# Moving six image measurements to VectorE, combining six more images and reordering the fifth one in a group-norm convolution

## The chip, the cores and the metric

The kernel runs on one core of a Trainium2 chip. The metric is the device time of one execution in microseconds (us). All runs of this study are marked fast in the record (none fell into a slower state), so they may be compared with each other. Single executions of one kernel lie up to about 2 us either side of its median. Part of that has one visible cause: the weights land at a slightly different time in each run, and the whole program shifts with them. Where traces are compared below, times are therefore also given *from the first product*, which is TensorE's first instruction, issued as soon as the range of the weights is known (17.71 us after the start of the span in the trace of before, 16.86 to 19.39 us in the others).

## The reference, cut to what matters

160 images of 128 channels and 32 x 32 pixels, five sets of weights of 32 images each, quantised in two levels on the way in. Every image is normalised per group of four channels, convolved 3 x 3, and added to itself.

```python
def _gn(v, G=32, eps=1e-5):
    g = v.reshape(B_, G, C_ // G, H_, W_)
    m = jnp.mean(g, axis=(2, 3, 4), keepdims=True)
    s = jnp.var(g, axis=(2, 3, 4), keepdims=True)
    return ((g - m) / jnp.sqrt(s + eps)).reshape(v.shape)

x = x + _L0_conv_ref(_gn(x), L0_conv_U)   # w = v1 + v2, two levels of floor()
```

## The kernel before

Every image is split into a high and a low float16 part, and TensorE convolves both. *Direct* images are normalised first (ScalarE: `z`, `hi`), and VectorE takes the low part and the row differences and sums (`lo`, `rows`). *Combined* images take differences and sums of rows first (`v`) and split afterwards (`vh` on ScalarE, `vl` on VectorE), which needs fewer products. Each image's mean and variance must be measured many steps ahead:

```python
def image(self, j, image):                 # by VectorE
    # ... half is 512 elements; st and both are small tiles
    for h in range(2):
        self.nc.vector.bn_stats(st[:, h, :], image[:, h * half : (h + 1) * half])
    self.nc.vector.bn_aggr(both, st)
    # ... two tiny products into mv

def image_sum(self, j, image, junk):       # by ScalarE, first pass
    self.nc.scalar.activation(junk, image, ACTF.Copy, scale=-1.0 / image.shape[1], accum_out=...)
def image_square(self, j, image, junk):    # by ScalarE, second pass
    self.nc.scalar.activation(junk, image, ACTF.Square, bias=..., accum_out=...)

def by_vector(self, i):
    return i >= self.EARLY and i % 8 in self.MEASURED      # MEASURED = (): nobody
def combined(self, i):
    return self.STEADY <= i < self.imgs - LAST and i % 8 in self.COMBINED   # STEADY = 14, LAST = 4
```

Step i finishes the convolution of image i. It begins with the products for the *next* image's sums of row pairs, into the one PSUM tile `m`. ScalarE copies half of it out (`leave`), VectorE makes the even and odd rows of the output from both halves (`pairs`, two instructions), and only then may TensorE overwrite `m` or go on with that image:

```python
def conv(self, i, on_the_way):
    if i + 1 < self.imgs:
        self.sums_of_pairs(i + 1)                # into m
    for halves in ((0,), (1,)) if i == self.imgs - 1 else ((0, 1),):
        for col in self.COLS:
            ...
            self.rest_of_column(i, col, halves)  # into eo

def leave(self, i):
    self.nc.scalar.copy(m2, self.m[i][:, 1])     # "m<-m" on ScalarE
def pairs(self, i):
    # ... m and m2 from leave(); rows are the even and odd rows of eo
    nc.vector.tensor_add(rows[:, :, 0], m[:, 0], m2)   # "eo<-m,m" on VectorE
    nc.vector.tensor_sub(rows[:, :, 1], m[:, 0], m2)
```

So a step's start needs, in this order: TensorE's sums, ScalarE's copy, VectorE's two instructions. The engines work through their queues in order, and what stands ahead of these in a queue delays TensorE.

Of the kernel before, what the change touches and what calls it, by code (L numbers as in the profile page):

```python
# [22 lines left out]
LAST = 4  # L23
# [109 lines left out]
def run(steps):  # L133

    while True:
        try:
            next(steps)
        except StopIteration as end:
            return end.value
# [170 lines left out]
class Main:  # L310
# [23 lines left out]

    STAT_LEAD = 14
    LOAD_LEAD = 20
    STEADY = 14
    COMBINED = (1, 3, 5, 7)
    MEASURED = ()
    EARLY = 8  # L340
    FIRST = 3

# [4 lines left out]
    def __init__(self, tc, ctx, keep, x, u, out):  # L347
        nc = self.nc = tc.nc
        self.imgs, C, self.H, self.W = x.shape
        P = self.P = nc.NUM_PARTITIONS  # L350
        assert C == P and self.H * self.W == 1024
        self.per_set = self.imgs // N_SETS
        self.xv = x.rearrange("(b n) c h w -> n c b (h w)", n=N_SETS)
        self.ov = out.rearrange("(b n) c h w -> n c b (h w)", n=N_SETS)
        self.uv = u.rearrange("n (o i k) -> n o i k", o=C, k=TAPS)

        def pool(name, bufs, **kw):
            return ctx.enter_context(tc.tile_pool(name=name, bufs=bufs, **kw))

        self.const = pool("const", 1)  # L360
        self.qpool = pool("quant", 1)
        self.wpool = pool("weights", 2)
        self.upool = pool("u", 1)
        self.xpool = pool("x", 12)
        self.zpool = pool("z", 3)
        self.parts = pool("parts", 4)
        self.rows = pool("rows", 4)
        self.wide = pool("wide", 1)
        self.wide_parts = pool("wide_parts", 2)
        self.evac = pool("evac", 2)  # L370
        self.sums = pool("sums", 4)
        self.unread = pool("unread", 1)
        self.small = pool("small", 3)
        self.ps_eo = pool("ps_eo", 2, space=PSUM)
        self.ps_m = pool("ps_m", 1, space=PSUM)
        self.ps_stat = pool("ps_stat", 1, space=PSUM)
        self.ps_tr = pool("ps_tr", 1, space=PSUM)
        self.steps = Steps(nc, keep)
        self.chunks, self.z, self.hi, self.v, self.eo, self.m = {}, {}, {}, {}, {}, {}
        self.sum = {}  # L380
        self.wts = {}
        self.columns = []

        cuts = [0, 2, 4, 8, 12, *range(16, self.imgs + 1, 8)]
        self.groups = [range(a, b) for a, b in zip(cuts, cuts[1:])]
        self.group_of = {i: k for k, g in enumerate(self.groups) for i in g}
        self.stats = {}
# [95 lines left out]


    def by_vector(self, i):
        return i >= self.EARLY and i % 8 in self.MEASURED

    def measure(self, i, stages=(0, 1)):

# [31 lines left out]

    def combined(self, i):

        return self.STEADY <= i < self.imgs - LAST and i % 8 in self.COMBINED

    def column_of(self, i):

# [95 lines left out]
    def banks(self, pool, tag, i):  # L623
        return pool.tile([self.P, 2, self.H // 2, self.W], F32, tag=tag, name=f"{tag}{i}")

    def direct_hi(self, i, col):

        if i not in self.eo:
            self.eo[i] = self.banks(*((self.ps_eo, "eo") if i < 2 else (self.ps_m, "m")), i)
        self.taps(i, (self.hi[i], 0), col, self.eo[i], False)  # L630
# [35 lines left out]
    def conv(self, i, on_the_way):  # L666


        if i + 1 < self.imgs:
            self.sums_of_pairs(i + 1)  # L670

        for halves in ((0,), (1,)) if i == self.imgs - 1 else ((0, 1),):
            for col in self.COLS:
                if col != self.COLS[0]:
                    on_the_way(col)
                self.rest_of_column(i, col, halves)
        del self.v[i]
# [64 lines left out]
    def run(self):  # L742
# [16 lines left out]
        warm = self.const.tile([P, 1], F32, tag="warm", name="warm")  # L759
# [22 lines left out]
        def take(steps, count):  # L782
            for _ in range(count):
                next(steps, None)
# [5 lines left out]
        def parts(i):  # L790
            self.normalise(i)
            self.high_part(i)
# [21 lines left out]
        measure(1, 3)  # L814
        self.stats[1].means()
        self.stats[1].deviations()
        parts(0)
        self.stats[1].variances()
        self.stats[1].deviation()
# [37 lines left out]
        for i in range(self.imgs):  # L857
            n, b = self.place(i)


            def on_the_way(col):
                if col == self.COLS[1]:
                    for st in ready:
                        st.means()
                    for *column, parts in self.columns:
                        turned.append((column, self.turn_column(*column, parts)))
                    self.columns.clear()
                if col == self.COLS[2]:
                    for st in middle:
                        st.variances()  # L870

            if i < self.FIRST:
                if i == self.FIRST - 1:
                    self.sums_of_pairs(self.FIRST)

                j = (i - 1) % self.FIRST
                self.direct_hi(j, self.COLS[2])
                self.direct_lo(j, self.COLS[2])
                if i == 0:
                    self.stats[2].variances()  # L880
                    self.stats[2].deviation()
                    self.stats[2].scales()
                for col in self.COLS:
                    on_the_way(col)
            else:
                j = i - 1
                self.conv(i, on_the_way)
            ahead = i + min(10 + i // 2, self.STAT_LEAD + 1)
            to_measure = range(measured, min(self.imgs, ahead))
            measured += len(to_measure)  # L890
            if n + 1 < N_SETS:
                if b == (2 if n == 0 else 0):
                    self.load_set(n + 1)
                if b == (4 if n == 0 else 2):
                    later = (s for col in self.COLS for s in self.make_column(n + 1, col))
            by_scalar = [k for k in to_measure if not self.by_vector(k)]


            direct = self.FIRST < i + 2 < self.imgs and not self.combined(i + 2)
            if i < self.FIRST:  # L900
                self.residual(j)
                if i == self.FIRST - 1:
                    self.leave(i + 1)
                    self.pairs(i + 1)
            if self.combined(i + 2):
                self.low_combined(i + 2)
            if direct:
                self.low_part(i + 2)
            take(later, 1)
            if direct:  # L910
                self.combinations(i + 2)
            if i > self.FIRST and self.by_hand(j):
                self.residual(j)
            for k in by_scalar:
                self.measure(k, (0,))
            if i > self.FIRST and not self.by_hand(j):
                self.residual(j)
                self.accumulate(j)
            if self.combined(i + 4):
                self.outer_rows(i + 4)  # L920


            if self.FIRST < i + 1 < self.imgs:
                self.leave(i + 1)
            if self.combined(i + 3):
                self.high_combined(i + 3)
            elif self.FIRST < i + 3 < self.imgs:
                self.normalise(i + 3)
                self.high_part(i + 3)
            for k in by_scalar:  # L930
                self.measure(k, (1,))
            for st in middle:
                st.deviation()
                st.scales()
            for st in ready:
                st.deviations()
            for column, pt in turned:
                self.keep_column(*column, pt)
            turned = []


            if self.FIRST < i + 1 < self.imgs:
                self.pairs(i + 1)
            if self.combined(i + 4):
                self.combine(i + 4)
            else:
                take(later, 1)
            if b == self.per_set - 4:
                run(later)

            middle, ready = ready, []
            for k in to_measure:
                if self.by_vector(k):
                    self.measure(k)
                group = self.group_of[k]
                if k + 1 == self.groups[group].stop:
                    ready.append(self.stats[group])
            self.store(i - 2)
            while loaded * NB < min(self.imgs, i + self.LOAD_LEAD):
                self.load(loaded)  # L960
                loaded += 1
# [49 lines left out]
```

## Time and profile before

| | before |
|---|---|
| time, median | 1011.69 us (1011.02 to 1012.54) |
| span of the profiled run | 1007.8 us |

In the profile PE is TensorE, PEld its loading of weights, DVE VectorE, ACT ScalarE and POOL GpSimd. The busy shares of the page (time, share, instructions), and two stretches of the first images, from the table of stretches of before (length, then busy time of PE, PEld, DVE, ACT, POOL, then TensorE's granted clock as a share of its full speed, DMA share, GB/s):

```profile
PE 964.8 (96%) x5910; PEld 575.6 (57%) x5910; DVE 886.5 (88%) x1197; ACT 931.2 (92%) x1279; POOL 369.5 (37%) x555
```

```profile
75.00:100.00 25.00, 25.00 (x145) 13.85 (x144) 16.28 (x28) 24.78 (x40) 9.80 (x19) 1.00 0.70 184
100.00:129.00 29.00, 27.11 (x154) 14.34 (x152) 19.41 (x34) 28.62 (x41) 4.17 (x7) 1.00 0.84 221
```

In both stretches ScalarE has 0.2 to 0.4 us left, and VectorE 9 us: a third of its time. That is the room that the change wants to use.

### The profile page before, as it was taken

What the parts mean: (1) busy time and instruction counts of PE and PEld (TensorE: products, weight loads), DVE (VectorE), ACT (ScalarE), POOL (GpSimd) and SP (SyncE); (2) the same over time, 40 slices, a digit from 0 to 9 for tenths busy, and PEclk for the clock granted to TensorE, in tenths of its full rate; (3) what the DMA queues carried; (4) which work ended last, traced back from release to release, by engine and by line L of the source; (5) the groups of instructions that cost most, each with busy time, mean ns of one, the idle gap of its engine ahead of it and who ended that gap; (6) DMA issues with size and microseconds to landing.
All of it is one profiled execution on the core that took longest, in us unless ns stands there. A gap on an engine that the chain in (4) does not pass through costs nothing.

```text
span 1007.8 us, 15892 instructions
## 1 busy us (share of the span) xinstructions
PE 964.8 (96%) x5910; PEld 575.6 (57%) x5910; DVE 886.5 (88%) x1197; ACT 931.2 (92%) x1279; POOL 369.5 (37%) x555
## 2 busy tenths in 40 slices
PE   1879999999999999999999999999999999999997
PEld 0435456665666665666666566666665666666663
DVE  7956689999999999989999999999999988888873
ACT  4899999999999999999999999999999999998660
POOL 3413162534425243524243444415243623333210
PEclk9989999999999999999999999999999999999999
DMA  9627889999999999999999999999999999997763
GB/s 361 238 84 188 210 233 260 261 260 270 270 274 293 272 270 261 257 274 286 269 290 260 266 265 277 291 286 262 264 254 262 289 266 275 268 256 191 180 176 129
DMA packets 67287, 254.42 MB, mean 252 GB/s; under 512 B 5248, under 2 KB 5248, under 8 KB 67200
## 3 DMA queue, kind: packets, MB, share of 16 engines
q1 hardware_dynamic: 45168, 173.09, 50.4%
q0 software_dynamic: 22032, 80.23, 40.9%
q8 instruction: 48, 0.79, 0.3%
q14 instruction: 39, 0.32, 0.1%
HBM read 89.19 MB, written 83.89 MB: 172 GB/s over the span
## 4 chain that ended last, share of the span: by engine, by line
PE 88%; ACT 7%; issue 2%; DVE 1%; POOL 1%; DMA 1%; SPq 0%
PE eo L614 30%; PE eo L640 28%; PE m L640 28%; ACT junk L199 2%; ACT z L511 1%; ACT junk L192 1%; ACT hi L519 1%; ACT sum L720 1%; DMA range<-in_L_conv_U_dram 1%; DVE ext L422 1%; DVE ext L423 1%; ACT m L696 0%; PE pg L225 0%; PE m L614 0%; PE pg L208 0%
## 5 line engine op out<-in xcount | busy, mean ns | idle before, releaser
L640 PEld LDWEIGHTS <-wt 128*128 128x128 f16 x4104 | 400.3, 98 | 240.1 <-DVE rows L590 7.8
L614 PE MATMUL eo<-hi,wt 128*128 128x496 f16 (+3 forms) x1584 | 381.8, 377 | 1.1 <-ACT wt L476 1.1
L733 POOL DMA_DIRECT2D xt<-sum x153 | 135.9, 888 | 462.8 <-ACT sum L720 443.1
L614 PEld LDWEIGHTS <-wt 128*128 128x128 f16 x1656 | 162.9, 100 | 156.7 <-issue 4.5
L199 ACT ACTIVATE junk<-xt,mv 128x1024 f16<-128x1024 f32 x160 | 183.3, 1146 | 0.4
L192 ACT ACTIVATE junk<-xt 128x1024 f16<-128x1024 f32 x160 | 169.1, 1057 | 14.1 <-DMA xt<-in_x_dram 10.7
L705 DVE TENSOR_TENSOR eo<-m,m 128x512 f32<-128x512 f32 x157 | 109.2, 696 | 76.2 <-ACT m L696 75.8
L567 DVE SCALAR_TENSOR_TENSOR vl<-v,rstd,vh 128x2048 f16<-128x2048 f32 x71 | 166.7, 2348 | 3.5 <-ACT vh L561 3.5
L720 ACT ACTIVATE sum<-eo 128x1024 f32<-128x1024 f32 x153 | 154.1, 1007 | 12.9 <-PE eo L640 12.9
L640 PE MATMUL eo<-vl,wt 128*128 128x248 f16 (+1 forms) x852 | 162.9, 273 | 0.0
L640 PE MATMUL eo<-vh,wt 128*128 128x248 f16 (+1 forms) x852 | 162.9, 273 | 0.0
L640 PE MATMUL m<-vh,wt 128*128 128x496 f16 (+1 forms) x426 | 161.8, 380 | 0.0
L640 PE MATMUL m<-vl,wt 128*128 128x496 f16 (+1 forms) x426 | 161.7, 380 | 0.0
L640 PE MATMUL eo<-rows,wt 128*128 128x248 f16 (+1 forms) x1032 | 155.6, 273 | 0.0
L561 ACT ACTIVATE vh<-v,rstd 128x2048 f16<-128x2048 f32 x71 | 143.0, 2014 | 0.0
L640 PE MATMUL m<-rows,wt 128*128 128x512 f16 x516 | 127.0, 383 | 9.5 <-DVE rows L590 7.3
L706 DVE TENSOR_TENSOR eo<-m,m 128x512 f32<-128x512 f32 x157 | 109.8, 700 | 5.4
L574 DVE TENSOR_TENSOR lo<-z,hi 128x1024 f16<-128x1024 f32 x89 | 108.9, 1224 | 5.9 <-ACT hi L519 5.8
L511 ACT ACTIVATE z<-xt,shift,rstd 128x1024 f32<-128x1024 f32 x89 | 110.7, 1244 | 1.3 <-POOL shift L242 1.3
L696 ACT COPY m<-m 128x512 f32<-128x512 f32 x157 | 91.2, 581 | 20.4 <-PE m L640 17.8
L519 ACT CAST hi<-z 128x1024 f16<-128x1024 f32 x89 | 93.0, 1045 | 2.8
L550 DVE TENSOR_TENSOR v<-xt 128x960 f32<-128x960 f32 x71 | 81.7, 1150 | 0.0
(105 smaller groups left out, 804.3 us busy)
## 6 DMA issues: line engine op xcount, KB each, us to landing
xt<-in_x_dram SPq DMA_DIRECT2D x78, 1024.0 KB, 9.1
out_dram<-xt SPq DMA_DIRECT2D x78, 1024.0 KB, 5.0
xt<-sum POOLq DMA_DIRECT2D x153, 512.0 KB, 6.8
range<-in_L_conv_U_dram SPq DMA_DIRECT2D x4, 576.0 KB, 6.9
u<-in_L_conv_U_dram SPq DMA_DIRECT2D x4, 576.0 KB, 11.5
xt<-in_x_dram SPq DMA_DIRECT2D x4, 512.0 KB, 9.4
out_dram<-xt SPq DMA_DIRECT2D x3, 512.0 KB, 3.0
u<-in_L_conv_U_dram SPq DMA_DIRECT2D x2, 288.0 KB, 3.1
```

The source lines that it names most:

```text
L192: self.nc.scalar.activation(junk, image, ACTF.Copy, scale=-1.0 / image.shape[1], accum_out=self.mv[:, j, 0:1],)
L199: self.nc.scalar.activation(junk, image, ACTF.Square, bias=self.mv[:, j, 0:1], accum_out=self.mv[:, j, 1:2],)
L511: nc.scalar.activation(z, self.image(i), ACTF.Identity, bias=st.shift[:, j : j + 1], scale=st.rstd[:, j : j + 1],)
L561: self.nc.scalar.mul(vh, self.v[i], st.rstd[:, j])
L567: self.nc.vector.scalar_tensor_tensor(vl, self.v[i], st.rstd[:, j], self.hi[i], ALU.mult, ALU.subtract)
L574: self.nc.vector.tensor_sub(lo[:, 1 : self.H + 1, :].rearrange("p h w -> p (h w)"), self.z.pop(i), self.hi[i].rearrange("p h w -> p (h w)"),)
L614: nc.tensor.matmul(target[:, h, r0 - h0 : r1 - h0, c0:c1], self.wts[n, col][:, k, :], tile[:, s0 : s0 + r1 - r0, c0 + dw : c1 + dw], start ...
L640: self.nc.tensor.matmul(target[:, :, c0:c1], self.wts[n, col][:, kind, :], source[:, :, c0 + dw : c1 + dw], start=start, stop=stop, skip_g ...
L705: nc.vector.tensor_add(rows[:, :, 0], m[:, 0], m2)
L706: nc.vector.tensor_sub(rows[:, :, 1], m[:, 0], m2)
L720: nc.scalar.mul(self.sum[i], eo, 0.5)
L733: self.nc.gpsimd.dma_start(self.image(i), self.sum.pop(i), accum_op=ALU.add)
```

## The change

Its intent: relieve ScalarE while the first images pass. Every second image of 8 to 19 is measured by VectorE. Images 7, 9, 11, 13 and, at the end, 157 and 159 are combined, which spares TensorE products. Step 3 starts with image 3's own first column, ahead of the next image's sums, and ScalarE's and VectorE's queues of steps 0 to 2 are reordered to match. Ten products of zeros before image 0 are to free TensorE's clock. The core of the diff:

```diff
-    STEADY = 14
-    COMBINED = (1, 3, 5, 7)
-    MEASURED = ()
+    STEADY = 7
+    MEASURED = 20
@@
     def by_vector(self, i):
-        return i >= self.EARLY and i % 8 in self.MEASURED
+        return self.EARLY <= i < self.MEASURED and i % 2 == 0
@@
     def combined(self, i):
-        return self.STEADY <= i < self.imgs - LAST and i % 8 in self.COMBINED
+        return self.STEADY <= i < self.imgs and i % 2 == 1
@@
+    def warm_up(self):
+        zeros = self.los[3].rearrange("p h w -> p (h w)")
+        target = self.banks(self.ps_m, "m", "warm")
+        for _ in range(10):
+            self.nc.tensor.matmul(..., zeros[:, :128], zeros[:, :512], start=True, stop=True)
@@ def conv(self, i, on_the_way):
-        if i + 1 < self.imgs:
+        if self.FIRST < i < self.imgs - 1:
             self.sums_of_pairs(i + 1)
@@
             for col in self.COLS:
+                if col == self.COLS[1] and i == self.FIRST:
+                    self.sums_of_pairs(i + 1)
@@ the loop, steps 0 to 2 (cut)
-                self.residual(j)
                 if i == self.FIRST - 1:
                     self.leave(i + 1)
                     self.pairs(i + 1)
+                    self.combinations(i + 2)
+                self.residual(j)
+                if i == self.FIRST - 2:
+                    self.low_part(i + 3)
+                for k in by_scalar:
+                    self.measure(k, (0,))
+                self.normalise(i + 4)
+                for k in by_scalar:
+                    self.measure(k, (1,))
+                self.high_part(i + 4)
... (from step 3 on as before; one more buffer for hi)
```

More of the change, by code (lines that the diff above doesn't have):

```diff
@@ L365, in __init__ @@
         self.zpool = pool("z", 3)
-        self.parts = pool("parts", 4)
+        self.parts = pool("parts", 5)
         self.rows = pool("rows", 4)
@@ L624, in banks @@
         return pool.tile([self.P, 2, self.H // 2, self.W], F32, tag=tag, name=f"{tag}{i}")
+    def warm_up(self):
+        zeros = self.los[3].rearrange("p h w -> p (h w)")
+        target = self.banks(self.ps_m, "m", "warm")
+        for _ in range(10):
+            self.nc.tensor.matmul(
+                target[:, 0].rearrange("p i w -> p (i w)"), zeros[:, :128], zeros[:, :512],
+                start=True, stop=True,
+            )
     def direct_hi(self, i, col):
@@ L673, in conv @@
             for col in self.COLS:
-                if col != self.COLS[0]:
+                if col == self.COLS[1] and i == self.FIRST:
+                    self.sums_of_pairs(i + 1)
+                if col != self.COLS[0] and halves[-1] == 1:
                     on_the_way(col)
@@ L816, in run @@
         self.stats[1].deviations()
+        self.warm_up()
         parts(0)
@@ L896, in run @@
             by_scalar = [k for k in to_measure if not self.by_vector(k)]
-            direct = self.FIRST < i + 2 < self.imgs and not self.combined(i + 2)
             if i < self.FIRST:
-                self.residual(j)
                 if i == self.FIRST - 1:
@@ L904, in run @@
                     self.pairs(i + 1)
-            if self.combined(i + 2):
-                self.low_combined(i + 2)
-            if direct:
-                self.low_part(i + 2)
-            take(later, 1)
-            if direct:
-                self.combinations(i + 2)
-            if i > self.FIRST and self.by_hand(j):
-                self.residual(j)
-            for k in by_scalar:
-                self.measure(k, (0,))
-            if i > self.FIRST and not self.by_hand(j):
-                self.residual(j)
-                self.accumulate(j)
@@ L919, in run @@
-            if self.combined(i + 4):
-                self.outer_rows(i + 4)
-            if self.FIRST < i + 1 < self.imgs:
-                self.leave(i + 1)
-            if self.combined(i + 3):
-                self.high_combined(i + 3)
-            elif self.FIRST < i + 3 < self.imgs:
-                self.normalise(i + 3)
-                self.high_part(i + 3)
-            for k in by_scalar:
-                self.measure(k, (1,))
+                    self.combinations(i + 2)
+                self.residual(j)
@@ new lines, in run @@
+                if i == self.FIRST - 2:
[6 more added lines that the diff above has]
+                self.high_part(i + 4)
+            else:
+                direct = i + 2 < self.imgs and not self.combined(i + 2)
+                if self.combined(i + 2):
+                    self.low_combined(i + 2)
+                if direct:
+                    self.low_part(i + 2)
+                take(later, 1)
+                if direct:
+                    self.combinations(i + 2)
+                if i > self.FIRST and self.by_hand(j):
+                    self.residual(j)
+                for k in by_scalar:
+                    self.measure(k, (0,))
+                if i > self.FIRST and not self.by_hand(j):
+                    self.residual(j)
+                    self.accumulate(j)
+                if self.combined(i + 4):
+                    self.outer_rows(i + 4)
+                if i + 1 < self.imgs:
+                    self.leave(i + 1)
+                if self.combined(i + 3):
+                    self.high_combined(i + 3)
+                elif self.FIRST + 3 < i + 3 < self.imgs:
+                    self.normalise(i + 3)
+                    self.high_part(i + 3)
+                for k in by_scalar:
+                    self.measure(k, (1,))
@@ L939, in run @@
             turned = []
-            if self.FIRST < i + 1 < self.imgs:
-                self.pairs(i + 1)
-            if self.combined(i + 4):
-                self.combine(i + 4)
-            else:
-                take(later, 1)
-            if b == self.per_set - 4:
-                run(later)
+            if i >= self.FIRST:
+                if i + 1 < self.imgs:
+                    self.pairs(i + 1)
+                if self.combined(i + 4):
+                    self.combine(i + 4)
+                else:
+                    take(later, 1)
+                if b == self.per_set - 4:
+                    run(later)
             middle, ready = ready, []
```

## The prediction

> **What bounds the kernel now.** I read the page's busy shares first, then a table of stretches, then the chain of waits between 55 and 145 us, then the timelines of TensorE and ScalarE there. The page says PE 96%, ACT 92%, DVE 88%: three engines near their limit, so an average cannot tell which one a change must relieve. The table of stretches does (stretch, its length, then busy time of PE, PEld, DVE, ACT, POOL, then TensorE's granted clock, DMA share, GB/s):
>
> ```profile
> 58.40:65.86 7.46, 0.18 (x1) 0.00 (x1) 4.83 (x7) 7.37 (x11) 0.00 (x0) 0.80 0.69 230
> 65.86:69.65 3.79, 3.79 (x9) 1.34 (x10) 2.87 (x5) 3.73 (x6) 0.00 (x0) 0.50 0.25 101
> 75.00:94.00 19.00, 19.00 (x113) 10.69 (x112) 12.43 (x22) 18.81 (x30) 6.96 (x14) 1.00 0.67 174
> 94.00:129.40 35.40, 33.24 (x187) 17.49 (x184) 23.66 (x40) 34.95 (x52) 7.21 (x11) 1.00 0.83 220
> 143.00:900.00 757.00, 757.00 (x4734) 459.57 (x4732) 704.90 (x926) 749.20 (x1022) 297.75 (x431) 1.00 1.00 271
> ```
>
> There are three regimes. From 58 to 66 us TensorE stands still while ScalarE is full, and the next 3.8 us run at half clock. From 94 to 129 us ScalarE is full (34.95 of 35.40) and TensorE has holes. From 143 us TensorE is full, ScalarE has 1% left and VectorE 7%. The timeline of TensorE shows the hole, the slow clock behind it, and three later image starts:
>
> ```profile
> 65.86 2.74 PE L640 MATMUL m<-rows,wt 128*128 128x512 f16 x6 [7.28 <-DVE rows L590]
> ...
> 93.97 1.46 PE L640 MATMUL m<-rows,wt 128*128 128x512 f16 x6
> ...
> 100.81 1.47 PE L640 MATMUL m<-rows,wt 128*128 128x512 f16 x6 [0.26 <-DVE eo L706]
> ...
> 107.92 1.47 PE L640 MATMUL m<-rows,wt 128*128 128x512 f16 x6 [0.52 <-DVE eo L706]
> ```
>
> The last three are steps 7, 8 and 9 (step i convolves image i): 6.84 and 7.11 us apart. How short could they be? At 976.26 us the same six products take 1.30 us to the next group, and the rest of a direct image 5.12 us (977.56 to 982.68): 6.42 us. A combined image takes 2.59 + 2.63 = 5.22 us (143.02 and 152.03 in the chain of work). So TensorE loses 0.4 to 0.7 us per image here. ScalarE's timeline of one step says to what:
>
> ```profile
> 101.41 1.15 ACT L199 ACTIVATE junk<-xt,mv 128x1024 f16<-128x1024 f32 x1
> 102.46 0.18 ACT L199 ACTIVATION_READ_ACCUMULATOR junk<-xt,mv 128x1 f32 x1
> 102.68 1.06 ACT L192 ACTIVATE junk<-xt 128x1024 f16<-128x1024 f32 x1
> 103.64 0.19 ACT L192 ACTIVATION_READ_ACCUMULATOR junk<-xt 128x1 f32 x1
> 103.86 1.06 ACT L192 ACTIVATE junk<-xt 128x1024 f16<-128x1024 f32 x1
> 104.82 0.19 ACT L192 ACTIVATION_READ_ACCUMULATOR junk<-xt 128x1 f32 x1
> 104.91 1.00 ACT L720 ACTIVATE sum<-eo 128x1024 f32<-128x1024 f32 x1
> 105.82 0.58 ACT L696 COPY m<-m 128x512 f32<-128x512 f32 x1
> 106.28 1.25 ACT L511 ACTIVATE z<-xt,shift,rstd 128x1024 f32<-128x1024 f32 x1
> 107.56 1.04 ACT L519 CAST hi<-z 128x1024 f16<-128x1024 f32 x1
> ```
>
> There is no gap. L192 and L199 measure images far ahead (up to two per step in steps 0 to 10, one afterwards); the copy m at L696, which lets TensorE's next image start, stands behind them.
>
> **What the skill says.** "TensorE: Matmul & The Clock Gate", section "Part 1: The HAM clock gate": the clock is halved by default, a window of about 3.4 us of work frees it, an idle one halves it again. The trace agrees: products start 0.42 us apart from 30.5 to 35.3 us and from 65.86 to 69.65 us, 0.216 us elsewhere. "ScalarE: Activation LUTs", section "What ACT_TABLE_LOAD costs": 186 ns + 0.833 ns per element, 93 ns more for a pointer operand. For 1024 elements that is 1039 and 1132 ns; the rows L192 and L199 have 1057 and 1146. "VectorE: DVE Perf Modes", section "The perf-mode tier table": reductions run at one element per cycle. It has no row for bn_stats. The trace has none either, but its maxima over 576 and 1152 elements take 748 and 1346 ns, 1.04 ns per element; so I estimate 0.62 us between starts for 512 elements, and M = 1.8 us for one image (two of them, an aggregate and two tiny products at 0.1 to 0.25 us each).
>
> **Part by part.** Starts are used, not durations, because rows overlap by 0.07 to 0.1 us.
>
> Zeros: ten products at the cold 0.427 us fill about 23.5 to 27.8 us, so image 0 starts warm at 30.51 us. That would save 12 x 0.21 = 2.5 us of TensorE, but the second weight column is ready by VectorE only at 39.30 us, unchanged. Worth 0; the wait grows by about 2 us.
>
> Fifth image: before, step 3 begins with the sums of image 4, which need z, hi, lo and rows of image 4 (rows until 66.1 us). After, step 3 begins with image 3's own column, which needs only L696 and L705/L706 of image 3. ScalarE's new queue, from the time 54.3 us when the shift of images 4 to 7 exists: z4 1.26, square of image 9 1.27, hi4 0.95, z5 1.26, hi5 0.95, so m3 at 60.0, sums on VectorE from 60.6 to 62.1. Step 3 starts at 62.15 us. TensorE idles 3.75 us instead of 7.3; before, the clock fell about 4.5 us into the hole (0.80 over that stretch), so I expect it to stay warm, which saves the 2 us at half clock.
>
> Measuring by vector: six images (8 to 18, even) leave ScalarE: 6 x 2.45 = 14.7 us. They cost VectorE 6 x 1.8 = 10.8 us. Combining 7, 9, 11, 13 saves TensorE 4 x 1.20 = 4.8 us, hardly changes ScalarE, and raises VectorE from 3.9 (lo 1.25, rows 1.3, sums 1.35) to 6.0 us an image (v 2.33, vl 2.28, sums 1.35). In steps 3 to 7 VectorE then has three combines, two vl, three low parts with rows, five sums, three measurements and six weight operations of 0.6: 35 us against 30.9 of TensorE (6.42 three times, 7.71, 3.93), and it starts them at 66, late by its work for images 8 to 12. So VectorE takes over the bound there. Laid out in order, with each queue's in-order work: step 4 starts at 70.2 (before 74.30), 5 at 76.6 (80.85), 6 at 83.2 (87.41), 7 at 91.8 (93.97), 8 at 98.1 (100.81), 9 at 105.8 (107.92), 10 at 109.8 (115.12), 11 at 117.5 (122.23). Then ScalarE binds once more, as steps 8 and 10 still measure two images each: the copy for image 12 comes at 121.7 us, so step 12 starts at 123.8 (129.43) where TensorE could have at 121.4. From there one measurement a step gives ScalarE 11.52 us per pair of images (340.25 to 351.77) against TensorE's 11.64. Step 13 starts at 131.5 (136.43), 14 at 135.4 (142.86), and step 15 at 143.1 against 142.86 + 7.71 = 150.57. The beginning gains 7.5 us. Both kernels do the same from image 16 to 156, and TensorE, full there, carries the gain through unchanged.
>
> End: 157 and 159 combined save 2 x 1.20 = 2.4 us. ScalarE measures nothing there any more, and VectorE makes no weights. VectorE's hand-made residuals (1.23 us each) fit between: the sums of image 159 are done 3 us before TensorE wants them. The tail after the last product, 7 us for the residual and the store, stays.
>
> Sum: 7.5 + 2.4 = 9.9 us of 1011.6; I predict 1001.7 us.
>
> **Rivals.** First, VectorE eats it: at 93% in the steady part it has 0.8 us free per pair, and a backlog built in steps 3 to 7 might last. If M is 3 us rather than 1.8, step 8 comes 2.5 to 3.5 us later and the start gains about 4 us: 1005. Against it: from step 8 on the pair costs VectorE 11.0 us, below 11.64. Second, ScalarE stays the bound until image 16 and further: its slack is only 0.12 us per pair, so steps 8 and 10 might push everything. My layout already has 2.35 us for this; doubled, 1004. Third, TensorE hardly waits at all, as 14.7 us less on ScalarE suggests: the hole and slow clock (3.7 + 2), the holes of steps 7 to 12 (3.9), the 4.8 and the 2.4 would add to 17 us: 995. Against it: the 35 against 30.9 us of VectorE in steps 3 to 7. Fourth, the clock falls in the 3.75 us hole: 2 us lost partly, as VectorE is the bound a little later; 1003.
>
> **Range and chances.** The beginning can gain 4 to 11 us, the end 1.5 to 2.5; the three runs spread by 1.5 us. So 997.5 to 1006 with 8 in 10. A 2% change needs 20 us, more than all the parts together could give even if none were hidden (17), so faster has 0.02. Slower needs a loss of 20 us that nothing in the queues suggests: 0.01.
>
> **What would show it.** Right: step 3's first product near 62 us at the full rate; bn_stats rows of about 0.6 us; waits of TensorE on VectorE's sums in steps 7 and 8, one behind L696 near step 12; step 15 at 143; the last product 9 to 10 us earlier. Wrong: products at 0.42 us spacing after 62 us; a bn_stats well over 0.7 us; TensorE waiting for ScalarE or VectorE all through the steady part; or less than 2 us gained after image 156.

## The result, and the profile after

| | before | after |
|---|---|---|
| median | 1011.69 us (1011.02 to 1012.54, 4 runs) | 1002.55 us (1001.74 to 1004.07, 4 runs) |
| ratio after/before | | 0.9911, 95% interval 0.9894 to 0.9928 |
| span of the profiled run | 1007.8 us | 1000.0 us |

The verdict is "same" at 2%; the kernel is 0.9% faster. Ratios here and below are the mean time of one kernel's fast runs over that of before's of the same rounds, so they are not quite the ratio of the medians that stand beside them. The two profiled runs differ by 7.8 us and the medians by 9.1: the profiled run of before (1009.54 us) was 2.1 us below the median of this set, that of after (1001.74 us) only 0.8 us. The traces can only explain the 7.8.

The same views of the kernel after: the busy shares, then the two stretches.

```profile
PE 959.1 (96%) x5920; PEld 576.2 (58%) x5920; DVE 906.7 (91%) x1227; ACT 916.5 (92%) x1249; POOL 374.4 (37%) x567
```

```profile
75.00:100.00 25.00, 23.01 (x138) 13.03 (x137) 24.66 (x43) 19.49 (x29) 9.84 (x19) 1.00 0.85 232
100.00:129.00 29.00, 26.97 (x164) 15.74 (x163) 25.78 (x36) 28.66 (x40) 7.79 (x13) 1.00 0.79 210
```

VectorE and ScalarE have changed places between 75 and 100 us: VectorE has 0.3 us left and ScalarE 5.5. TensorE, full before, now waits 2 us there. From 100 to 129 us ScalarE is full again. All waits of over 1 us in TensorE's timeline after 60 us and up to 235 us (the bracket holds the idle time ahead of a row and what ended it):

```profile
62.40 1.44 PE L613 MATMUL eo<-hi,wt 128*128 128x512 f16 x6 [3.30 <-DVE eo L718]
...
70.43 1.47 PE L650 MATMUL m<-rows,wt 128*128 128x512 f16 x6 [1.29 <-DVE eo L718]
...
97.66 0.39 PE L650 MATMUL m<-vh,wt 128*128 128x512 f16 x1 [1.92 <-DVE eo L718]
...
123.43 0.39 PE L650 MATMUL m<-vh,wt 128*128 128x512 f16 x1 [2.03 <-DVE eo L718]
...
148.49 0.39 PE L650 MATMUL m<-vh,wt 128*128 128x512 f16 x1 [1.30 <-DVE eo L718]
```

These are the starts of steps 3, 4, 8, 12 and 16. All name VectorE's second `pairs` instruction (L718), the last in the order above, so each must be followed further back. At step 4 it is VectorE's own queue. Here is the measurement that stands in it, from VectorE's timeline:

```profile
64.66 1.27 DVE L182 BATCH_NORM_STATS2 st<-xt 128x6 f32<-128x512 f32 x2
65.97 0.21 DVE L184 BATCH_NORM_AGGREGATE both<-st 128x2 f32<-128x12 f32 x1
66.28 0.15 DVE L185 TENSOR_SCALAR mv<-both 128x1 f32<-128x1 f32 x1
66.35 0.14 DVE L186 TENSOR_SCALAR mv<-both 128x1 f32<-128x1 f32 x1
66.41 1.22 DVE L573 TENSOR_TENSOR lo<-z,hi 128x1024 f16<-128x1024 f32 x1
```

The two `bn_stats`, over 512 elements each, take 1.31 us (65.97 - 64.66; their starts are 0.60 us apart), a whole measurement 66.41 - 64.66 = 1.75 us here, and between 1.68 us (59.24 to 60.92) and 1.81 us (53.49 to 55.30) elsewhere. At step 16, VectorE waits for ScalarE's copy `m` (L708), and ScalarE had waited for GpSimd two images earlier. Three rows of ScalarE and GpSimd, in order of time:

```profile
131.02 2.96 POOL L235 TENSOR_TENSOR rstd<-ve,mhalf 128x8 f32<-128x8 f32 x1 [1.79 <-ACT ve L231]
```

```profile
134.72 1.24 ACT L510 ACTIVATE z<-xt,shift,rstd 128x1024 f32<-128x1024 f32 x1 [1.29 <-POOL shift L242]
...
146.39 0.58 ACT L708 COPY m<-m 128x512 f32<-128x512 f32 x1
```

The inverse square root of eight images' variances takes GpSimd 2.96 us; ScalarE stands still for 1.29 us behind it at 134.72, and from there on it is full until its copy for step 16 at 146.39, which TensorE awaits. Before had the same stop of ScalarE, 1.32 us at 141.43, but TensorE was late enough there to see nothing of it. No run took the stop away, so how much of the wait it causes is argued, not shown.

The gain along the program, as starts of steps in the two traces (step 3 begins with other products in after, see the change):

| step | before | after | predicted | gain |
|---|---|---|---|---|
| 3 | 65.86 | 62.40 | 62.15 | 3.5 |
| 4 | 74.30 | 70.43 | 70.2 | 3.9 |
| 8 | 100.81 | 97.66 | 98.1 | 3.2 |
| 12 | 129.43 | 123.43 | 123.8 | 6.0 |
| 14 | 142.86 | 135.38 | 135.4 | 7.5 |
| 15 | 150.57 | 143.10 | 143.1 | 7.5 |
| 16 | 154.58 | 148.49 | gain kept | 6.1 |
| 30 | 236.99 | 231.68 | gain kept | 5.3 |
| 156 | 976.26 | 970.83 | gain kept | 5.4 |
| last residual | 1000.85 | 993.02 | | 7.8 |

### The profile page after: what moved, and what is told of

Same layout as the page of the kernel before. It is cut to its first block, busy times and chain, and to the rows that moved or that the text cites. A ratio compares the mean times of both kernels' runs of the same rounds, so it can differ in the third digit from the quotient of the medians.

```text
span 1000.0 us, 15935 instructions
## 1 busy us (share of the span) xinstructions
PE 959.1 (96%) x5920; PEld 576.2 (58%) x5920; DVE 906.7 (91%) x1227; ACT 916.5 (92%) x1249; POOL 374.4 (37%) x567
## 4 chain that ended last, share of the span: by engine, by line
PE 82%; DVE 8%; ACT 6%; issue 2%; DMA 1%; POOL 1%; SPq 0%; DVEq 0%; ACTq 0%
PE eo L613 27%; PE m L650 27%; PE eo L650 27%; ACT junk L199 2%; ACT vh L560 1%; ACT sum L732 1%; PE m L613 1%; DVE lo L573 1%; DVE eo L717 1%; DVE eo L718 1%; ACT m L708 1%; ACT z L510 1%; DVE vl L566 1%; DVE st L182 1%; DMA range<-in_L_conv_U_dram 1%
## 5 line engine op out<-in xcount | busy, mean ns | idle before, releaser
L613 PE MATMUL eo<-hi,wt 128*128 128x496 f16 (+1 forms) x1476 | 355.0, 377 | 4.6 <-DVE eo L718 3.3
L566 DVE SCALAR_TENSOR_TENSOR vl<-v,rstd,vh 128x2048 f16<-128x2048 f32 x77 | 180.8, 2347 | 3.1 <-ACT vh L560 3.1
L650 PE MATMUL m<-vh,wt 128*128 128x496 f16 (+1 forms) x462 | 175.5, 380 | 5.9 <-DVE eo L718 5.9
L650 PE MATMUL eo<-vl,wt 128*128 128x256 f16 (+1 forms) x924 | 177.1, 273 | 0.0
L650 PE MATMUL eo<-vh,wt 128*128 128x256 f16 (+1 forms) x924 | 177.1, 273 | 0.0
L650 PE MATMUL m<-vl,wt 128*128 128x496 f16 (+1 forms) x462 | 175.4, 380 | 0.0
L560 ACT ACTIVATE vh<-v,rstd 128x2048 f16<-128x2048 f32 x77 | 155.0, 2013 | 0.3 <-DVE v L555 0.3
L650 PE MATMUL eo<-rows,wt 128*128 128x248 f16 (+1 forms) x960 | 144.3, 273 | 0.0
L650 PE MATMUL m<-rows,wt 128*128 128x496 f16 (+1 forms) x480 | 116.9, 380 | 1.4 <-DVE eo L718 1.3
L718 DVE TENSOR_TENSOR eo<-m,m 128x512 f32<-128x512 f32 x157 | 109.8, 699 | 5.4
L708 ACT COPY m<-m 128x512 f32<-128x512 f32 x157 | 91.2, 581 | 25.3 <-PE m L650 22.4
L510 ACT ACTIVATE z<-xt,shift,rstd 128x1024 f32<-128x1024 f32 x83 | 103.2, 1244 | 2.6 <-POOL shift L242 2.6
```

The source lines that it names most:

```text
L510: nc.scalar.activation(z, self.image(i), ACTF.Identity, bias=st.shift[:, j : j + 1], scale=st.rstd[:, j : j + 1],)
L560: self.nc.scalar.mul(vh, self.v[i], st.rstd[:, j])
L566: self.nc.vector.scalar_tensor_tensor(vl, self.v[i], st.rstd[:, j], self.hi[i], ALU.mult, ALU.subtract)
L613: nc.tensor.matmul(target[:, h, r0 - h0 : r1 - h0, c0:c1], self.wts[n, col][:, k, :], tile[:, s0 : s0 + r1 - r0, c0 + dw : c1 + dw], start ...
L650: self.nc.tensor.matmul(target[:, :, c0:c1], self.wts[n, col][:, kind, :], source[:, :, c0 + dw : c1 + dw], start=start, stop=stop, skip_g ...
```

## The experiments

Twelve kernels ran beside before and after, in five sets, each set on one chip with runs of before. Compare kernels of different sets by their ratios first: the median of before moves from 1010.1 to 1011.7 us between the sets. "From the first product" are the columns on the right: starts of step 4, 8, 12, 16 and 158 in the trace of each kernel.

| kernel | median us | ratio to before (95%) | 4 | 8 | 12 | 16 | 158 |
|---|---|---|---|---|---|---|---|
| before | | 1 | 56.59 | 83.10 | 111.72 | 136.87 | 971.39 |
| after | 1002.55 | 0.9911 (0.9894 to 0.9928) | 52.54 | 79.77 | 105.54 | 130.60 | 964.58 |
| e1, no zeros | 1002.24 | 0.9903 (0.9888 to 0.9918) | 52.50 | 79.72 | 105.52 | 130.59 | 964.69 |
| e2, no vector measuring | 1007.24 | 0.9958 (0.9943 to 0.9973) | 56.26 | 82.73 | 110.74 | 135.81 | 969.90 |
| e3, 7 to 13 direct | 1000.90 | 0.9895 (0.9880 to 0.9910) | 52.47 | 78.57 | 104.56 | 129.50 | 962.71 |
| e4, 157 and 159 direct | 1005.33 | 0.9938 (0.9925 to 0.9952) | 52.73 | 79.71 | 105.51 | 130.93 | 966.45 |
| e8, order alone | 1010.33 | 0.9998 (0.9989 to 1.0007) | 57.29 | 83.39 | 111.04 | 136.17 | 970.59 |
| e9, vector measuring alone | 1005.74 | 0.9943 (0.9927 to 0.9960) | 55.22 | 81.32 | 107.30 | 132.25 | 967.86 |
| e10, combining 7 to 13 alone | 1010.28 | 0.9993 (0.9984 to 1.0002) | 56.98 | 82.76 | 110.72 | 135.78 | 971.14 |
| e13, all but order and zeros | 1003.63 | 0.9926 (0.9912 to 0.9939) | 54.01 | 79.27 | 106.55 | 131.95 | 966.45 |
| e7, other six measured, no zeros | 997.63 | 0.9872 (0.9855 to 0.9888) | 52.50 | 77.41 | 102.85 | 126.47 | 960.62 |
| e11, e7 with 7 to 13 direct | 1001.00 | 0.9904 (0.9887 to 0.9920) | 52.69 | 78.79 | 104.78 | 129.39 | 963.25 |
| e12, e7 with image 12 later | 997.65 | 0.9867 (0.9851 to 0.9884) | 52.58 | 77.83 | 103.28 | 126.89 | 960.86 |
| e14, e7 with the hole filled | 998.45 | 0.9884 (0.9867 to 0.9900) | 52.50 | 77.40 | 102.85 | 126.46 | 960.40 |

The theory at the outset was the prediction's: VectorE's measuring is the useful part, the order helps, the zeros are worth nothing, combining spares TensorE 1.2 us an image, and the end 2.4 us. The rivals stand in the expectation of each run.

### One part undone

**e1, without the zeros.**

```diff
         self.stats[1].deviations()
-        self.warm_up()
```

> The changed kernel without the ten products of zeros. My theory: they end at 27.2 us, the clock falls again at about 29.8 us in the pause that follows, and image 0 starts at half clock anyway; they only delay the statistics by 0.5 us. Without them every step start from 3 to 15 comes 0.4 to 0.6 us earlier and the time falls by 0.5 us, to about 1002. Rival (the intent): the zeros keep the clock up, and without them the time rises by 1 to 2.5 us.

Measured: 1002.24 us against 1002.55, and every start from the first product within 0.11 us of after's. The zeros are worth nothing that these runs can resolve. The half microsecond that the expectation wanted to gain at the steps did not come. How the zeros work can be seen in TensorE's timeline of e2, which has them; the second row below is image 0 at the full rate (12 products in 2.74 us), but TensorE then waits for ScalarE:

```profile
22.45 4.43 PE L631 MATMUL mwarm<-lo 128*128 128x512 f16 x10
...
29.50 2.74 PE L613 MATMUL eo<-hi,wt 128*128 128x512 f16 x12 [1.42 <-ACT wt L475]
33.59 1.43 PE L613 MATMUL m<-hi,wt 128*128 128x512 f16 x6 [1.34 <-ACT hi L518]
```

In after's own trace the zeros didn't even do that: image 0's twelve products took 5.20 us, half rate, since the clock had fallen again at 29.69 us, in the pause behind the zeros. The later starts were the same with warm and with cold products.

**e2, nobody measured by VectorE.**

```diff
     def by_vector(self, i):
-        return self.EARLY <= i < self.MEASURED and i % 2 == 0
+        return False
```

> The changed kernel with images 8 to 18 measured by ScalarE. Theory: ScalarE has about 8 us of waits between 52 and 97 us into which the 14.7 us partly fit; the remaining 6 us delay step 12 from 123.4 to about 129 us: time about 1008. Rival: VectorE is the bound there, so that freeing it of 10.8 us makes up for the loss: within 1 us of the changed kernel.

Measured: 1007.24 us, 4.7 us slower than after and 5.2 us later at step 12. The theory held: about half of the gain hangs on moving the measurements.

**e3, images 7 to 13 direct.**

```diff
-    STEADY = 7
+    STEADY = 14
```

> The changed kernel with images 7, 9, 11, 13 direct as before. Theory: VectorE and ScalarE set the pace of steps 4 to 12, so of the 4.8 us that TensorE spares only about 1 us is seen: 1003.5, step 12 near 123.5 to 124 us as in the changed kernel, step 15 about 1 us later. Rival: TensorE is what binds there, and the whole 4.8 us are lost: 1007.3.

Both missed: at 1000.90 us it is *faster* than after by 1.6 us (1.9 us in the traces at step 158). The intervals of the ratios overlap, but the traces agree from step 8 on. The stretches of e3:

```profile
75.00:100.00 25.00, 25.00 (x147) 14.01 (x146) 22.38 (x46) 21.27 (x32) 9.36 (x16) 1.00 0.86 235
100.00:129.00 29.00, 29.00 (x169) 16.13 (x168) 21.74 (x36) 28.68 (x42) 7.51 (x14) 1.00 0.86 221
```

TensorE has no hole in either stretch: it does the 4.8 us of products that combining spares, in the time that after spends waiting. VectorE has room again (22.38 of 25, 21.74 of 29). Combined images put `v` and `vl`, about 2.3 us each, on VectorE where direct ones have `lo` and `rows`, 2.5 us together, and in after VectorE was the full engine. So after reaches step 8 1.2 us later than e3. ScalarE, which decides steps 12 to 16, starts that much later: from its copy for step 12 to its copy for step 16 it needs 146.39 - 121.33 = 25.06 us in after and 145.60 - 120.47 = 25.13 us in e3. It can't catch up, and step 16 is 1.1 us later for having combined. (e3's ScalarE has the same stop behind GpSimd, 1.31 us at 134.56, and TensorE doesn't wait for it.) Most of the rest up to step 158 comes at step 30, where after waits 0.62 us and e3 does not; the part on the prediction returns to it.

**e4, images 157 and 159 direct.**

```diff
-        return self.STEADY <= i < self.imgs and i % 2 == 1
+        return self.STEADY <= i < self.imgs - LAST and i % 2 == 1
```

> The changed kernel with images 157 and 159 direct as before. Theory: TensorE is full to the end, so the time rises by 2 x 1.20 = 2.4 us to 1005, with all of it after step 155. Rival: the end is set by VectorE's residuals and the stores, and the time rises by under 1 us.

Measured: 1005.33 us, 2.8 us slower, against 2.4 expected. The theory held, within the scatter. Its trace showed something else. Up to image 150 it is the same program as after, and at step 12 TensorE waits equally long, 2.05 and 2.03 us. But the granted clock behind that wait differed. Rows of the table of stretches (granted clock third from the right), e4 first, then after:

```profile
124.00:128.00 4.00, 4.00 (x12) 1.49 (x11) 4.00 (x7) 3.53 (x7) 2.18 (x3) 0.57 1.00 295
```

```profile
124.00:128.00 4.00, 4.00 (x23) 2.00 (x21) 4.00 (x8) 4.00 (x9) 2.35 (x4) 1.00 0.99 296
```

In e4 TensorE got through 12 products in the four microseconds, in after through 23. Step 13 came 1.7 us later for it; ScalarE's bound at step 16 hid all but 0.3 us. The instructions are the same, so the clock can fall in such a hole in one run and hold in another. The clock records of the traces say what differs. The clock changes only on a grid of 3.41 us (in e4 at 66.07, 124.09 and 127.51 us: 17 spacings, then one), and the grid lies differently in each trace. e4's hole, 121.54 to 123.59, lies whole in one spacing, and the clock is halved at its end (1.00, then 0.50); after's hole, 121.40 to 123.43, is cut in two at 121.85, and the clock holds. First two spacings of e4, then the two of after:

```profile
120.68:124.09 3.41, 1.36 (x11) 0.78 (x10) 1.95 (x3) 3.38 (x5) 1.44 (x3) 1.00 0.89 286
124.09:127.50 3.41, 3.41 (x10) 1.20 (x9) 3.41 (x6) 3.41 (x7) 1.76 (x3) 0.50 0.98 293
```

```profile
118.43:121.85 3.42, 2.97 (x27) 2.40 (x25) 1.36 (x2) 3.39 (x7) 0.12 (x1) 1.00 0.40 128
121.85:125.26 3.41, 1.83 (x9) 0.89 (x10) 3.29 (x5) 3.38 (x6) 1.31 (x3) 1.00 0.98 274
```

So TensorE is idle for 2.05 us of one spacing in e4, and for 0.45 and 1.58 us of two in after. Counted over all fourteen traces from 45 us to 960 us, the clock was halved at the end of all fourteen full-speed spacings with 2.03 us of idle time or more, and of none with 1.99 us or less. (Before 45 us, where many products are tiny, this does not hold: it fell once behind 1.70 us.)

### One part alone

**e8, the order alone** (after without zeros, without vector measuring, with 7 to 13, 157 and 159 direct).

```diff
-    STEADY = 7
+    STEADY = 14
...
-        return self.EARLY <= i < self.MEASURED and i % 2 == 0
+        return False
...
-        return self.STEADY <= i < self.imgs and i % 2 == 1
+        return self.STEADY <= i < self.imgs - LAST and i % 2 == 1
...
-        self.warm_up()
```

> The other order for the fifth image alone: nothing measured by VectorE, nothing newly combined, no zeros. Theory: step 3 starts near 62 us at full clock, 3.7 us and a cold stretch earlier than before, but ScalarE has the same work without a gap from there to step 13, so step 13 comes within 1 us of the kernel before (136.4) and the time is 1010 to 1011.7. Rival: the 4 to 5.7 us stay: 1006 to 1007.5.

Measured: 0.9998, and step 13 at 136.28 us, as the theory said. Its other half missed: step 3 did not start near 62 us at full clock but at 66.04, with six products in 2.69 us. The hole ahead of it was 6.74 us against 7.28 before, because ScalarE's copy stands behind measurements:

```profile
63.95 0.57 ACT L708 COPY m<-m 128x512 f32<-128x512 f32 x1
```

**e9, vector measuring alone** (from the kernel before).

```diff
-        return i >= self.EARLY and i % 8 in self.MEASURED
+        return self.EARLY <= i < 20 and i % 2 == 0
```

> The kernel before with only images 8 to 18 (even) measured by VectorE. Theory: this relieves ScalarE, which set the start of step 3 as well as the pace up to step 13: step 3 near 60.5 us instead of 65.86, step 14 5 to 7 us earlier, time about 1005 to 1006.5, most of the gain of the beginning. Rival: without the other order it does nothing to the hole, and the time falls by 2 to 3 us only.

Measured: 1005.74 us, as expected in time: this one line brings 5 to 6 us of the 9. The start of step 3 was missed, 64.28 us, later than expected; the hole shrank from 7.28 to 4.84 us, and the products behind it still ran at half rate (six in 2.74 us).

**e10, combining 7 to 13 alone** (from the kernel before, `STEADY = 7`).

> The kernel before with only images 7, 9, 11, 13 combined in addition. Theory: ScalarE sets the pace there and its work hardly changes, so the 4.8 us that TensorE spares are not seen: 1010.5 to 1012. Rival: TensorE binds: 1007.

Measured: 0.9993. Step 16 comes 1.1 us earlier and step 158 only 0.25 us. With ScalarE full, TensorE's spared products become waits.

**e13, everything but the order and the zeros** (from the kernel before).

```diff
-    STEADY = 14
+    STEADY = 7
...
+        return self.EARLY <= i < 20 and i % 2 == 0      # by_vector
...
+        return self.STEADY <= i < self.imgs and i % 8 in self.COMBINED
```

> The kernel before with every part of the change but the order of the fifth image and the zeros: images 8 to 18 (even) measured by VectorE, images 7 to 13, 157 and 159 combined. It tells what the order is worth beside the other parts. Theory: the order is worth about 2 us once the measurements have left ScalarE (the difference between the vector part alone plus the end, about 1002.9, and the changed kernel with 7 to 13 direct, 1000.9), so this kernel takes about 1004.5. Rival, the prediction's step: the order spares 3.5 us of hole and 2 us of slow clock, so this kernel takes 1006 or more. Second rival: it is hidden, as it was alone, and this kernel takes 1002.5 as the changed one.

Measured: 1003.63 us, between the theory's 1004.5 and the second rival's 1002.5. Against after and e1 (1002.55 and 1002.24) the order, with the one more buffer that e13 lacks too, is worth 1.1 to 1.4 us in the medians and 1.5 to 2.3 us by the ratios, whose intervals overlap; it is 1.9 us at step 158 in the traces, part of which may again be the clock: in this trace too it fell at step 12, behind a hole of 2.03 us. It is not the 5.5 us that the hole and the slow clock cost TensorE: VectorE's queue, not TensorE, sets step 4. The same order alone was worth nothing (e8), so its worth depends on the measurements having left ScalarE.

### Is it the choice of images? e7 and its variants

In after ScalarE measures two images in each of the steps 8 and 10, and none or one in the steps in which VectorE is full. So I chose other six images: 14 and 16, measured while VectorE is full and ScalarE has 5.5 us free, go back to ScalarE; 20 and 24, measured in steps 8 and 10, go to VectorE. The zeros are left out.

```diff
-        return self.EARLY <= i < self.MEASURED and i % 2 == 0
+        return i in (8, 10, 12, 18, 20, 24)
...
-        self.warm_up()
```

> The changed kernel without zeros, with VectorE measuring images 8, 10, 12, 18, 20, 24 in place of 8, 10, 12, 14, 16, 18. Theory: in steps 4 and 5 VectorE is the bound and ScalarE waits 3.5 us, in steps 8 to 11 ScalarE is the bound and VectorE waits 3 us; moving three measurements swaps the work to who is free. Step 8 at about 95 us (97.7 in the changed kernel), step 12 at 120.5 (123.4), step 16 at 144 (148.5), time about 997.5 to 998.5. Rival: only the number of images measured by VectorE matters, and the time stays within 1 us of 1002.5.

Measured: 997.63 us, as expected. It beats before by 1.3%, and after by 4 to 5 us (3.9 by the ratios, 4.9 by the medians, 4.0 in the traces at step 158), with the same amount of work. What is left of TensorE's waits after step 3 in its timeline up to 160 us:

```profile
107.14 0.39 PE L650 MATMUL m<-vh,wt 128*128 128x512 f16 x1 [0.76 <-DVE eo L718]
...
120.01 0.39 PE L650 MATMUL m<-vh,wt 128*128 128x512 f16 x1 [0.92 <-DVE eo L718]
```

Steps 8 and 16 no longer wait, and steps 10 and 12 wait less than 1 us each, where after had 1.92 us at step 8, 2.03 at 12 and 1.30 at 16. (Step 4 starts where it did; e12 and e14 look at it.) This shows that it was the two queues that set the pace, and that the places of the six measurements decide how far.

**e11, e7 with 7 to 13 direct** (`STEADY = 14`).

> The kernel of the run with the other six measured images (no zeros; VectorE measures 8, 10, 12, 18, 20, 24), but with images 7 to 13 computed directly. Theory: with the measurements moved out of VectorE's full stretch, TensorE is the bound from step 8 on, so combining pays: this one is slower than 997.6 us by about 2 (999.5 to 1000), and step 16 starts about 2 us later from the first product (128.4 in place of 126.5). Rival: combining costs here as it did with six measurements packed between 8 and 18, so this one is faster (about 996).

Measured: 1001.00 us, 3.4 us slower than e7 (2.6 us in the traces at step 158), and 2.9 us later at step 16. Combining, which cost 1.6 us in after, pays about 3 us here. Its stretches say why: TensorE is now the full engine, 25.00 of 25 and 29.00 of 29, with VectorE and ScalarE below it in both.

```profile
75.00:100.00 25.00, 25.00 (x144) 13.86 (x143) 20.22 (x37) 24.17 (x38) 10.74 (x16) 1.00 0.85 229
100.00:129.00 29.00, 29.00 (x170) 16.31 (x169) 26.91 (x48) 27.95 (x39) 8.71 (x15) 1.00 0.91 240
```

**e12, e7 with image 12 measured a step later.**

```diff
+            if i == self.FIRST:
+                self.measure(12)
             middle, ready = ready, []
             for k in to_measure:
-                if self.by_vector(k):
+                if self.by_vector(k) and k != 12:
```

> The same six measured images, but image 12's vector measurement is done at the end of step 3 and no longer in step 2, ahead of the first residual. Theory: VectorE's queue sets step 4's start; taking one measurement (1.8 us) out of the queue ahead of it starts step 4 about 1.3 us earlier from the first product (51.1 in place of 52.5) and the time falls to about 996.3. Rival: the measurement only moves behind, VectorE is full until step 9 anyway, and step 8 on stands where it stood: 997.6, the same.

Measured: 997.65 us, as the rival said; step 4 from the first product at 52.58. It did not test the theory cleanly, though. VectorE's queue got shorter, but in the traces of e12 and e7 the clock fell in the hole ahead of step 3, so TensorE itself was busy until step 4. First TensorE's two rows (six products in 2.54 us; step 4 without a wait), then VectorE's, which now waits for ScalarE's copy:

```profile
62.72 2.54 PE L613 MATMUL eo<-hi,wt 128*128 128x512 f16 x6 [3.29 <-DVE eo L718]
...
70.97 1.46 PE L650 MATMUL m<-rows,wt 128*128 128x512 f16 x6
```

```profile
68.23 0.70 DVE L717 TENSOR_TENSOR eo<-m,m 128x512 f32<-128x512 f32 x1 [0.65 <-ACT m L708]
```

**e14, e7 with the hole filled.** So the clock had to be kept up in the hole, with 18 products that nobody reads:

```diff
+                if i == self.FIRST - 1:
+                    idle = self.ps_tr.tile([P, ROW * P], F32, tag="pt", name="idle")
+                    for _ in range(18):
+                        nc.tensor.matmul(idle, self.wts[0, 1][:, 0, :], ...hi[3]..., start=True, stop=True)
```

> The kernel with the other six measured images, with 18 products of 384 columns, whose result nobody reads, put into TensorE's hole ahead of step 3 (about 3 us of the 3.3), so that the clock can't fall there. In the traces of this kernel with and without image 12's measurement moved, the first products after the hole ran at half rate and TensorE was back to back until step 4, which hid whatever the moved measurement was worth. Theory: the slow clock costs nothing, because VectorE's sums for step 4 end when TensorE does: step 3's products run at the full rate, TensorE waits about 1.3 us for VectorE at step 4 in its place, step 4 and step 8 start as before from the first product (52.5 and 77.4), 997.6 us. Rival, the fourth of the prediction: the slow products cost 1 to 2 us, and this kernel takes about 996.5.

The theory held, to 0.02 us at steps 4, 8, 12 and 16. The clock stays up, and TensorE waits instead:

```profile
60.41 3.09 PE L900 MATMUL idle<-hi,wt 128*128 128x384 f16 x18
63.86 1.44 PE L613 MATMUL eo<-hi,wt 128*128 128x512 f16 x6 [0.36 <-DVE eo L718]
...
71.89 1.47 PE L650 MATMUL m<-rows,wt 128*128 128x512 f16 x6 [1.29 <-DVE eo L718]
```

What the slow products took reappears as a wait of 1.29 us for VectorE: from step 3 to step 4 it is 8.02 us in e7 and 8.03 us here. The time, 998.45 us, is 0.8 us above e7's with overlapping intervals; its first product came 2.2 us later than e7's in the traces, and step 158 from there 0.2 us earlier. With e12 it follows that step 4 has several bounds that lie within about a microsecond of each other. Moving image 12's measurement *and* filling the hole together was not tried.

## Why the prediction was right

The predicted 1001.7 us stands against a median of 1002.55, well inside the range.

- **Zeros, worth 0:** right (e1). Image 0, which the prediction has warm, ran warm in the traces of e2, e3 and e4 and cold in after's own, with the same steps after it; what was spared turned into a wait, as the prediction had it.
- **Step 3 at 62.15 us at the full rate:** 62.40, six products in 1.44 us. The hole was 3.30 us (3.75 predicted). "I expect it to stay warm" was luck: with a hole of 3.29 or 3.30 us the clock held in the traces of after and e1, where the grid cut the hole (1.31 and 1.99 us, 1.76 and 1.54 us), and fell in those of e3, e4, e7, e11 and e12, where 2.79 to 3.29 us of it lay in one spacing. It did not matter for the time, since VectorE sets step 4; e14 shows that.
- **M = 1.8 us, VectorE the bound in steps 3 to 7:** right. A measurement took 1.68 to 1.81 us, VectorE was busy 24.66 of 25 us, and the starts of steps 4, 8, 12, 14 and 15 fell within 0.5 us of the predicted ones. The first rival, VectorE eating the gain until 1005 us, fell with M; the third, TensorE hardly waiting, with steps 4, 8, 12 and 16.
- **ScalarE binds once more at step 12:** right (123.43 against 123.8, wait 2.03). e7, which takes its double measurements of steps 8 and 10 away, starts step 12 2.7 us earlier from the first product.
- **"Both kernels do the same from image 16 to 156, and TensorE, full there, carries the gain through unchanged":** this step failed. TensorE was not full there: it waited 1.30 us at step 16 and 0.62 us at step 30. Of 7.5 us at step 15, 1.4 were gone at step 16 and 0.8 more by step 30; 5.4 arrived at step 156. At step 16 the trace shows ScalarE, stopped for 1.29 us by GpSimd's inverse square root and full from there on: the second rival in small. The prediction gave ScalarE 11.52 us a pair, so 23.04 us for the two pairs up to step 16; between its copies for steps 12 and 16 it needed 25.06, and the difference is the stop of 1.29 us and 0.75 us of making weights (138.09 to 138.84). The stop was in the profile of before, 1.32 us at 141.43 us, hidden only because TensorE was later. The wait at step 30 is for VectorE, while the next set's weights are made, and it comes with combining 7 to 13: it is 0.61 to 0.63 us in all nine traces in which they are combined, and absent in all five in which they are direct (before, e3, e8, e9, e11). In the loop a combined image takes the place of one of VectorE's pieces of weight making (`take(later, 1)`), and what is left over is done at once in step 28 (`run(later)`): five pieces, 225.17 to 227.94 us, in after, and two, 224.28 to 225.14 us, in e3. The general mistake: a row without a wait in the profile of before is not proof that there is slack.
- **End, 2.4 us:** right. 7.8 at the last residual less 5.4 at step 156 is 2.4; e4 gave 2.8 in the medians, part of which is its clock.
- **Sum:** 7.5 + 2.4 = 9.9 predicted; the traces have 7.5 - 2.1 + 2.4 = 7.8, the medians 9.1 (the interval of the ratio allows 7.3 to 10.7). That the medians came within 1 us of the 9.9 therefore does not make up for the step that failed: 2.1 us of the gain were lost on the way.
- **Combining 7 to 13 as a saving of 4.8 us of TensorE:** right as arithmetic, and wrong as a benefit. The prediction's layout has those images without asking what it would be with them direct. e3 shows that here it cost 1.6 us.
- **The order:** its two gains, the shorter hole and the 2 us at half clock, were never summed alone, and could not have been: alone 0 (e8), with the rest 1 to 2 us (e13).

## What to carry to other kernels

When two engines share the bound, the worth of a part has no fixed sign: combining four images was worth 0 alone, -1.6 us beside measurements that had filled VectorE, and about +3 us once the same number of measurements had been spread over the steps in which each engine had room. So lay out the queues step by step, move work to the steps in which the receiving engine is idle, and test each part with the others present. A gain made early is carried through a full stretch only up to the next chain that TensorE's lateness had been hiding.

## What the Trainium skill lacked or had wrong

- "TensorE: Matmul & The Clock Gate", section "HAM oscillation — how this bites in real kernels", gives as a rule that idle gaps should not exceed about 3.4 us. Here gaps of 2.05, 2.03 and 2.17 us (e4 and e13 at step 12, e10 at step 10) were followed by half the clock for 3.41 us, while gaps of 2.03 us in after and up to 2.19 us in e2 left it at 1.00; gaps of 3.3 us went either way (held in two traces, fell in five). What decided was the idle time within one spacing of the 3.41 us grid: halved from 2.03 us on, held up to 1.99 us. A gap shorter than the rule's is not safe here. The section "Part 1: The HAM clock gate" tells of variation from run to run at the warm-up; these runs show it for falling, too.
- "VectorE: DVE Perf Modes", section "The perf-mode tier table", has no row for bn_stats: 0.60 us from start to start for 512 float32 elements per partition, 1.68 to 1.81 us in after for one whole measurement of 1024, against 2.45 us for the two passes on ScalarE.
- No page that I found gives GpSimd's time for a power: 1.04 to 2.38 us for 128x4 elements, 1.67 to 3.02 us for 128x8 over all traces. In after one of these (2.96 us) stands ahead of ScalarE's stop of 1.29 us before step 16.
